# Layer 2's gate and up values by 26 products of a joint table, with GpSimd multiplying silu(gate) by up

## The chip, the core and the metric

The kernel runs on one core of a Trainium2 chip. The core's engines each work through their own instructions in order and wait for each other by semaphores: TensorE (PE, with its weight loads shown apart as PEld), VectorE (DVE), ScalarE (ACT), GpSimd (POOL) and SyncE (SP), whose queue issues all the DMA transfers spoken of here. Matrix products are written to PSUM and must be read out from there by VectorE or ScalarE. The metric is the device time of one execution in microseconds (us), all in float32.

## What is computed

x has 4 x 512 = 2048 rows of 512; the weights W_gate, W_up are 1376 x 512, W_down 512 x 1376, and each layer has its own. Cut to what matters:

```python
def layer1(x):                       # the k = 688 smallest |s| of a row become zero
    s = silu(x @ w_gate.T)
    s = zero_smallest_half(abs(s), s)
    return (s * (x @ w_up.T)) @ w_down.T
def layer2(x):
    return (silu(x @ W_gate.T) * (x @ W_up.T)) @ W_down.T
x = x + layernorm(layer1(layernorm(x)))
x = x + layernorm(layer2(layernorm(x)))
```

## The kernel before

The 2048 rows are 16 tiles of 128 rows. The program is one stretch of unrolled code; a scheduler of the language orders each engine's instructions by its own timeline estimate, within what `tc.issue_after` fixes by hand, and tile pools decide which tensors share memory: `big` has ten buffers (tag "b5"), `work` mostly two for a tag, and PSUM has the tags pa, px, py and pt with two banks each. A second path, `general`, is in the program for rows that the search could not settle and does not run here.

*Seven products.* Most matrix products use the scheme of seven products for a 2 x 2 x 2 block product (`Seven`, L134 to L168): sums of blocks are formed ahead (`stationary_sums` L117 for the weights' side, `moving_sums` L125 for the other), seven block products are accumulated in three banks, and while they run VectorE and ScalarE read partial sums out of the banks and add them up (`first`, `second`, `third`). A block product is two matmuls over 128 of the 512 inner values each (L144).

*Layer 1* runs over 8 units of two tiles (`units`, the loop over `j`): gate products (L433), up products by the seven-product scheme, a search for each row's threshold in six counting steps (L485 to L510 on ScalarE and VectorE), transposes of the masked values (`turns`, L607), sums of blocks (`down_sums` L618, on VectorE, tile D) and the down products (`finish`, which calls `downs` L234, with products p1 to p7), then the layer norm and the residual (`out_norm` L344). The units are overlapped: unit j's gate and up products carry the transposes of unit j-2 and the down products of unit j-3.

*The weights' sums* of the seven-product scheme are formed early in layer 1 by `presum` (L180): it loads blocks of a weight, forms four sums on VectorE with operations of 128 x 1280, and stores them to DRAM (`presums`). The first unit does this for layer 1's down weight ("a"), the second for layer 2's down, gate and up weights ("f", "g", "u"). At the end of layer 1 the sums of gate and up are loaded into the places that layer 1's weights held (tags wg, wu, and extra tiles).

*Layer 2* runs over 4 blocks of four tiles, 512 rows each. `Block.norm` normalizes and transposes a tile into xT; `Block.sums` forms the four sums of the moving side (4 operations of 128 x 512). The first 1280 of the 1376 hidden values go in five groups (HC = 5) of two slices of 128 hidden values: `Block.pair` (L682) makes gate and up values for a group, each with its own seven products of two matmuls of 256 columns, 28 matmuls in all, takes silu on ScalarE (L697, L700) and multiplies by up on VectorE (L698, L702). `Block.down_sums` (L721) forms the group's sums for the down product on GpSimd (four operations of 128 x 256, L119 to L122, tiles hTb and D). `Block.rest` does the last 96 hidden values with 14 matmuls. Then `Block.finish` does the down products for the block's tiles and the output norm. The norms and sums of the next block are issued behind the last group's last product (`block.mark`), under the down products.

*Around the change of layers* the program's order is: block 0's norms, the weights' loads, block 0's sums, the last unit's transposes, its block sums, its down products, and then the groups; TensorE's order as scheduled puts the first products of block 0 among the last unit's transposes and down products.

The lines that the steps below touch: L144, L154, L160, L161, L167, L168 (products and read-outs of `Seven`; L153 is ScalarE's first read-out), L260 and L266 (down products), L373 and L607 (transposes), L104 to L110 and L358, L359 (norms), L119 to L130 (sums), L206 and after (`presum`).

Of the kernel before, what the change touches and what calls it, by code (L numbers as in the profile page):

```python
# [29 lines left out]

@with_exitstack
def sandwich_kernel(
# [10 lines left out]
):  # L43

# [20 lines left out]
    HC = FULL // 2  # L65
    HF = HC * P
# [26 lines left out]
    presums = {k: dram.tile([4, P, HC * H2], F32, name=f"sum_{k}") for k in ("a", "f", "g", "u")}  # L93
# [86 lines left out]
    def presum(work, key, w_d):  # L180


        down = key in "af"
        bufs = dict(wd=3, hT=2)

        def load(r, c, tag, k):
            t = work.tile([P, HC * H2], F32, tag=tag, name=f"ps_{key}_{k}", bufs=bufs[tag])
            if down:
                src = w_d[r * HF : (r + 1) * HF, c * H2 : (c + 1) * H2]
            else:  # L190
                src = w_d[c * 2 * P : (c + 1) * 2 * P, r * HF : (r + 1) * HF]
            n = HC if down else 2
            nc.sync.dma_start(
                t.rearrange("p (k h) -> p k h", k=n), src.rearrange("(k p) h -> p k h", p=P)
            )
            return t

        def keep(k, t):
            nc.sync.dma_start(presums[key][k - 1], t)

        x = load(0, 1, "wd", "x") if down else load(1, 0, "wd", "x")
        y = load(0, 0, "wd", "y") if down else load(1, 1, "wd", "y")
        z = load(1, 1, "hT", "z") if down else load(0, 0, "hT", "z")
        w = load(1, 0, "wd", "w") if down else load(0, 1, "wd", "w")
        if down:
            nc.vector.tensor_sub(y, x, y)  # L206
        else:
            nc.vector.tensor_add(y, x, y)
        keep(1, y)
        nc.vector.tensor_sub(x, z, x)  # L210
        keep(3, x)
        if down:
            nc.vector.tensor_sub(z, z, y)
        else:
            nc.vector.tensor_sub(z, y, z)
        keep(2, z)
        nc.vector.tensor_sub(w, w, z)
        keep(4, w)

# [157 lines left out]
    class Unit:  # L377
# [205 lines left out]
        def turns(self, other=False):  # L583
# [4 lines left out]
            def turn(k, g0):  # L588
                nm = f"{self.nm}_{self.tiles[k]}"
                if g0 == 0:  # L590
                    if other:
                        if k == 0:
                            self.ends = self.work.tile(
                                [P, 2, P], F32, tag="S", name=f"he{nm}", bufs=1
                            )
                        t = self.big.tile([P, 2 * HC, P], F32, tag="b5", name=f"hT{nm}")
                        end = self.ends[:, k, :]
                    else:
                        t = self.work.tile([P, NI, P], F32, tag="hT", name=f"hT{nm}")
                        end = t[:, NI - 1, :]  # L600
                    self.hT.append((t, end[: isz[-1], :]))
                h, (hT, end) = self.p[k], self.hT[k]
                n = min(4, NI - g0)
                pt = psum.tile([P, 4, P], F32, tag="pt", name=f"ph{nm}_{g0}")
                for c in range(n):
                    i = g0 + c
                    nc.tensor.transpose(  # L607
                        pt[: isz[i], c, :], h[:, i * P : i * P + isz[i]], ident
                    )
                nf = n if g0 + n <= FULL else n - 1  # L610
                copy = nc.vector.tensor_copy if other and k else nc.scalar.copy
                copy(hT[:, g0 : g0 + nf, :], pt[:, :nf, :])
                if nf < n:
                    copy(end, pt[: isz[-1], nf, :])
# [39 lines left out]
    class Block:  # L654
# [15 lines left out]
        def sums(self):  # L670
            t = [
                self.big.tile([P, 2, 2, N2], F32, tag="b5", name=f"T{self.nm}_{self.b}_{q}")
                for q in range(2)
            ]
            self.right = moving_sums(
                nc.vector,
                *[half[:, :, cols] for half in self.xT for cols in (slice(N2), slice(N2, N))],
                t[0][:, 0], t[0][:, 1], t[1][:, 0], t[1][:, 1],
            )
            self.h = []  # L680

        def pair(self, a, lefts):  # L682
# [6 lines left out]
            sg = self.work.tile([P, 4, N2], F32, tag="w", name=f"sg{nm}", bufs=1)  # L689
            ms = []  # L690
            for k, left, c in zip("gu", lefts, (sg, h)):
                left = {p: w[:, :, ts(a, P)] for p, w in left.items()}
                m = Seven(f"{k}b{nm}", left, self.right, c[:, 1, :], c[:, 2, :], c[:, 3, :])
                m.first()
                ms.append(m)
            c11g, c11u = [m.second() for m in ms]
            nc.scalar.activation(sg[:, 0, :], c11g, AF.Silu)  # L697
            nc.vector.tensor_mul(h[:, 0, :], sg[:, 0, :], c11u)  # L698
            ms[0].third()
            nc.scalar.activation(sg[:, 1:, :], sg[:, 1:, :], AF.Silu)  # L700
            ms[1].third()
            self.mark = nc.vector.tensor_mul(h[:, 1:, :], sg[:, 1:, :], h[:, 1:, :]).ins  # L702

        def rest(self, left):

            n = I - 2 * HF
            nm = f"{self.nm}_{self.b}"
            t = self.work.tile([P, 4, N2], F32, tag="w", name=f"sgr{nm}", bufs=1)[:n]
            m = Seven(f"rb{nm}", left, self.right, t[:, 0, :], t[:, 1, :], t[:, 2, :])
            m.first()  # L710
            c11 = m.second()
            h = self.big.tile([P, N], F32, tag="b5", name=f"hTb{nm}_r")
            lo, hi = h[:n, :N2], h[:n, N2:]
            nc.scalar.activation(lo, c11, AF.Silu)
            m.third()
            nc.scalar.activation(hi, m.c12, AF.Silu)
            nc.vector.tensor_mul(lo, lo, m.c21)
            nc.vector.tensor_mul(hi, hi, m.c22)
            self.h.append(h)
# [17 lines left out]
        def finish(self, which, wr, final=False):  # L737

            pairs = []
            for q in which:  # L740
                last = lambda i, q=q: self.h[-1][: isz[-1], ts(q + 2 * i, P)]
# [23 lines left out]
    def layers(nm, general):  # L765
        with ExitStack() as sctx:
# [4 lines left out]
            def extra(k, layer):  # L771
                return [
                    wpool.tile([P, 2, 2 * Q], F32, tag=f"w{k}s{q}", name=f"w{k}s{q}{layer}{nm}")
                    for q in range(3)
                ]

# [23 lines left out]
            t1, t2, t4 = extra("u", 1)  # L800
# [23 lines left out]
            else:  # L824
                wr = last_rows(a_wd, 1)
                w_ds = dict(a=a_wd, f=f_wd, g=f_wg, u=f_wu)
                sums_at = {0: "a", 1: "fgu"}
                for j in range(NU):
# [22 lines left out]
                    for k in sums_at.get(j, ""):  # L851
                        presum(work, k, w_ds[k])
                steps = finish(units[-3:-1], wr)
# [14 lines left out]
            lefts, ws = [], []  # L868
            for k, w_d in (("g", f_wg), ("u", f_wu)):
                w = wpool.tile([P, NH, I], F32, tag="w" + k, name=f"w{k}2{nm}")  # L870
                s1, s2, s4 = [y[:, :, :HF] for y in extra(k, 2)]
                a11, a12, a21, a22 = [
                    w[:, 2 * c : 2 * c + 2, r * HF : (r + 1) * HF] for r in range(2) for c in range(2)
                ]
                for q, a in ((1, s1), (2, s2), (3, a21), (4, s4)):
                    nc.sync.dma_start(a, presums[k][q - 1].rearrange("p (k h) -> p k h", k=2))
                for a, c, r in ((a11, 0, 0), (a12, 1, 0), (a22, 1, 1)):
                    nc.sync.dma_start(
                        a,
                        w_d[c * 2 * P : (c + 1) * 2 * P, r * HF : (r + 1) * HF].rearrange(  # L880
                            "(k p) h -> p k h", p=P
                        ),
                    )
                nc.sync.dma_start(
                    w[:, :, 2 * HF :], w_d[:, 2 * HF :].rearrange("(k p) h -> p k h", p=P)
                )
                lefts.append(dict(p1=a11, p2=a12, p3=s4, p4=a22, p5=s1, p6=s2, p7=a21))
                ws.append(w)
            blocks[0].sums()
            if not general:  # L890
                for f in units[-1].turns():
                    f()
                units[-1].down_sums()
                for f in finish([units[-1]], wr):
                    f()
            wr = last_rows(f_wd, 2)
            t = work.tile([P, 3, 2, I - 2 * HF], F32, tag="S", name=f"wrs{nm}", bufs=1)
            rest = stationary_sums(
                nc.vector,
                *[w[:, 2 * c : 2 * c + 2, 2 * HF :] for w in ws for c in range(2)],  # L900
                t[:, 0], t[:, 1], t[:, 2],
            )
            for b, block in enumerate(blocks):
                last = b + 1 == len(blocks)
                for a in range(HC):
                    block.pair(a, lefts)
# [3 lines left out]
                block.rest(rest)  # L910
# [53 lines left out]
```

## Time and profile before

| | us |
|---|---|
| median of 3 runs | 867.67 (867.36 to 868.07) |
| the profiled execution | 867.17 |
| its span in the profile | 865.39 |
| layer 2, first product of block 0 alone to the span's end | about 445 to 865 |
| period of a block of layer 2 | 102.3 |

In the profile a line names engine, source line, operation, output <- inputs (partitions x elements), and count. A float32 matmul is two passes and counts twice: `x160` are 80 matmuls. The mean length of a matmul (380 ns for a pass of 256 columns) is its latency; passes follow each other more closely than that, so their spacing is read from the timeline. The costliest groups of layer 2 and some of the others:

```profile
L433 PE MATMUL pg<-wg,xT 128*128 128x456 f32 (+1 forms) x384 | 154.8, 549 | 0.2 <-ACT p L437 0.2
L144 PE MATMUL paub<-xTb,wu 128*128 128x256 f32 x160 | 41.3, 380 | 0.1
L144 PE MATMUL pagb<-xTb,wg 128*128 128x256 f32 x160 | 41.1, 379 | 0.0
L119 POOL TENSOR_TENSOR D<-hTb 128x256 f32<-128x256 f32 x20 | 14.6, 729 | 193.9 <-DVE hTb L702 193.9
L700 ACT ACTIVATE sg<-sg 128x768 f32<-128x768 f32 x20 | 16.9, 843 | 50.3 <-DVE sg L168 50.3
```

The figures behind the bar are the group's busy time, the mean of one in ns, and the idle time of the engine before them with what ended most of it.

### The profile page before, as it was taken

Reading aid. Unit: us, or ns where it says so; the run is one execution under the profiler, and the core shown is the slowest. Engines: PE = TensorE matmul, PEld = TensorE weight load, DVE = VectorE, ACT = ScalarE, POOL = GpSimd, SP = SyncE. Lnnn points to the kernel's source line nnn. Section 1 sums busy time; section 2 is a strip of 40 time slices with the busy share of each in tenths; the row PEclk is TensorE's granted clock in tenths of the full one; section 3 lists DMA queues with packets and bytes.
Section 4 is the critical chain, followed back from the end, with each engine's and each line's share of the span. In section 5 each row is a group of like instructions: output and inputs, shape, how many; then the busy total and the mean of one; then the engine's idle time right before and its main releaser. Section 6 shows DMA issues by size and latency. Waiting matters only on the chain.

```text
span 865.4 us, 10342 instructions
## 1 busy us (share of the span) xinstructions
PE 854.2 (99%) x3642; PEld 659.6 (76%) x3642; DVE 533.7 (62%) x1432; ACT 302.5 (35%) x601; POOL 98.8 (11%) x178
## 2 busy tenths in 40 slices
PE   9999999999999999999999999999999999999996
PEld 5556566767667676677888888888888888888885
DVE  5887787776949677667955445544436445454434
ACT  3465575647474755656111111011111112011100
POOL 1000000000000001000001220121301222012111
PEclk9999999999999999999999999999999999999999
DMA  9999414334233333387573005500054001430032
GB/s 334 372 329 347 177 55 123 122 100 163 67 116 108 123 122 104 100 323 262 169 242 119 0 1 170 189 2 0 18 183 159 1 0 46 153 125 1 0 100 100
DMA packets 60381, 112.96 MB, mean 131 GB/s; under 512 B 4705, under 2 KB 34529, under 8 KB 60321
## 3 DMA queue, kind: packets, MB, share of 16 engines
q1 hardware_dynamic: 60176, 111.95, 38.4%
q8 instruction: 31, 0.51, 0.2%
q14 instruction: 30, 0.24, 0.1%
q10 hardware_dynamic: 144, 0.26, 0.1%
HBM read 93.32 MB, written 18.87 MB: 130 GB/s over the span
## 4 chain that ended last, share of the span: by engine, by line
PE 51%; DVE 2%; ACT 1%; DMA 1%; issue 0%; POOL 0%; ACTq 0%; DVEq 0%
PE pxub L144 6%; PE pxgb L144 6%; PE pxdb L260 6%; PE paub L144 4%; PE pagb L144 4%; PE pydb L260 4%; PE pyub L144 4%; PE pygb L144 4%; PE padb L260 3%; PE pxd L260 2%; PE pyd L260 2%; PE pxrb L144 1%; PE pad L260 1%; ACT ja L485 1%; PE parb L144 1%; PE ptb L373 1%
## 5 line engine op out<-in xcount | busy, mean ns | idle before, releaser
L485 ACT ACTIVATE ja<-v,cur 128x1376 bf16<-128x1376 f32 x96 | 138.4, 1441 | 64.1 <-DVE cur L510 43.0
L433 PE MATMUL pg<-wg,xT 128*128 128x456 f32 (+1 forms) x384 | 154.8, 549 | 0.2 <-ACT p L437 0.2
L433 PEld LDWEIGHTS pg<-wg,xT 128*128 128x128 f32 x384 | 71.9, 190 | 62.7 <-issue 57.6
L144 PE MATMUL pau<-wu,xT 128*128 128x344 f32 x128 | 43.1, 453 | 0.0
L144 PE MATMUL paub<-xTb,wu 128*128 128x256 f32 x160 | 41.3, 380 | 0.1
L144 PE MATMUL pagb<-xTb,wg 128*128 128x256 f32 x160 | 41.1, 379 | 0.0
L144 PE MATMUL pxub<-T,wu 128*128 128x256 f32 x160 | 41.1, 379 | 0.0
L144 PE MATMUL pxgb<-T,wg 128*128 128x256 f32 x160 | 41.1, 379 | 0.0
L260 PE MATMUL pad<-wd_p,hT 128*128 128x256 f32 x160 | 38.9, 380 | 0.1
L437 ACT ACTIVATE p<-pg 128x456 f32<-128x456 f32 (+1 forms) x48 | 26.0, 543 | 36.4 <-PE pg L433 33.1
L260 PE MATMUL pydb<-wdb_p,D 128*128 128x256 f32 x160 | 37.3, 379 | 0.0
L490 DVE TENSOR_SCALAR low<-cur 128x2 int32<-128x2 f32 x48 | 7.9, 165 | 47.1 <-ACT ja L485 46.7
L260 PE MATMUL pxd<-wd_p,hT 128*128 128x256 f32 x160 | 36.8, 379 | 0.0
L119 POOL TENSOR_TENSOR D<-hTb 128x256 f32<-128x256 f32 x20 | 14.6, 729 | 193.9 <-DVE hTb L702 193.9
L260 PE MATMUL padb<-wdb_p,hTb 128*128 128x256 f32 x160 | 36.7, 379 | 0.0
L260 PE MATMUL pxdb<-wdb_p,hTb 128*128 128x256 f32 x160 | 36.2, 379 | 0.0
L260 PEld LDWEIGHTS pad<-wd_p,hT 128*128 128x128 f32 x160 | 29.9, 190 | 6.7 <-DMA wd_p<-in_L_attn_w_down_dram 0.5
L260 PEld LDWEIGHTS pxd<-wd_p,hT 128*128 128x128 f32 x160 | 30.4, 190 | 5.5 <-issue 0.4
L700 ACT ACTIVATE sg<-sg 128x768 f32<-128x768 f32 x20 | 16.9, 843 | 50.3 <-DVE sg L168 50.3
L110 POOL TENSOR_TENSOR rs_o<-ve_o,nhalf 128x1 f32<-128x1 f32 x16 | 11.5, 731 | 198.0 <-DVE ve_o L108 198.0
L144 PEld LDWEIGHTS paub<-xTb,wu 128*128 128x128 f32 x160 | 30.3, 190 | 4.5 <-ACT sg L697 0.4
L260 PEld LDWEIGHTS pxdb<-wdb_p,hTb 128*128 128x128 f32 x160 | 30.4, 190 | 4.2
(245 smaller groups left out, 1699.5 us busy)
## 6 DMA issues: line engine op xcount, KB each, us to landing
wd_p<-sum_a SPq DMA_DIRECT2D x28, 640.0 KB, 4.0
wd_p<-in_L_attn_w_down_dram SPq DMA_DIRECT2D x21, 640.0 KB, 3.9
wdb_p<-sum_f SPq DMA_DIRECT2D x16, 640.0 KB, 4.0
wdb_p<-in_L_ffn_W_down_dram SPq DMA_DIRECT2D x12, 640.0 KB, 3.9
xn<-in_x_dram SPq DMA_DIRECT2D x16, 256.0 KB, 4.1
xr<-in_x_dram SPq DMA_DIRECT2D x16, 256.0 KB, 4.1
x<-y SPq DMA_DIRECT2D x16, 256.0 KB, 3.1
xnb<-x SPq DMA_DIRECT2D x16, 256.0 KB, 4.1
```

The lines of the kernel that those rows point to most:

```text
L110: nc.gpsimd.tensor_tensor(rs, ve, nhalf, ALU.pow)
L119: eng.tensor_add(s1, a21, a22)
L144: nc.tensor.matmul(ps, self.left[k][:, c, :], self.right[k][:, c, :], start=first and c == 0, stop=c == 1, skip_group_check=not first,)
L260: nc.tensor.matmul(p[which], p[1](k, c), ws[k][:, c, :], start=first and c == 0, stop=c == HC - 1, skip_group_check=not first,)
L373: nc.tensor.transpose(pt[:, c, :], xn[:, ts(c, P)], ident)
L433: nc.tensor.matmul(pg, self.xT[:, i, c, :], wg[:, c, c0:c1], start=(c == 0), stop=(c == NH - 1),)
L437: nc.scalar.activation(p[:, c0:c1], pg, AF.Silu)
L485: nc.scalar.activation(junk, v, AF.Sign, bias=cur[:, 0, i : i + 1], accum_out=cur[:, 1, i : i + 1],)
L490: nc.vector.tensor_scalar(low, cur[:, 1, :], 0.0, None, ALU.is_gt)
L700: nc.scalar.activation(sg[:, 1:, :], sg[:, 1:, :], AF.Silu)
```

## The change

Layer 2's gate and up values of a group are no longer two times seven products of 2 x 2 x 2 blocks, but one table of 26 products for blocks of 4 (inner) x 2 (halves of the rows) x 2 (slices), found for gate and up together: each product is a single matmul of a sum of weight blocks (128 x 128) with a sum of blocks of x (128 x 256).

- `LEFT_SUMS` are the 18 sums of x's blocks, formed once for each block by `Block.sums` on VectorE, each 128 x 256. `RIGHT_SUMS` are the steps that turn a group's 16 weight blocks into 26, on VectorE in layer 1 (`weight_sums`): 17 steps for each group, 15 over two blocks (256 columns) and 2 over one, in units 0 to 4 for groups 4 to 0. Groups 4 to 1 are stored to DRAM (`w_ops`) and loaded at the end of layer 1; group 0's stay in memory (`area`).
- `PRODUCTS` lists, for each product, one of six banks, the index of the weight operand, that of the operand of x, and the outputs (0 to 3 gate, 4 to 7 up) to which the bank's content is added or subtracted after it. A bank used again accumulates. Outputs' first values are written by ScalarE, 8 for a group; the 18 additions are VectorE's.
- When a slice's gate is complete, ScalarE takes its silu (512 columns); GpSimd multiplies it by the up values (512 columns, two for a group) in place of VectorE's L698 and L702.
- The products of a block are ordered by hand (`issue_after`) in the order of the table.
- `Block.rest` does its 96 hidden values directly: 8 matmuls of 512 columns, one silu, one product on VectorE. Block 0's is issued before the last unit's down products.
- `presum` of "g" and "u" is gone, and the sums of the rest's weights.
- Block 0's sums are issued behind the last unit's block sums. The tile `he` gets a tag of its own; `sg` alternates between two tags, and the rest's hTb is in tag "junk".

The diff, cut to its core:

```diff
+LEFT_SUMS = (
+    "0 - 1", "2 - 6", "0 - 3", "5 - 6", "4 - 8", "6 - 7", "4 - 10", "5 + 9",
...
+RIGHT_SUMS = (
+    "2,16 = 2,12 - 6,8", "17,23 = 8,9 + 9,10", "18,19 = 11,11 + 17,23", "10,21 = 10,12 - 6,17",
...
+PRODUCTS = (
+    (0, 10, 17, "+2"), (1, 13, 23, "+6"), (2, 14, 24, "+1"), (0, 25, 21, "+6"), (1, 24, 8, "+2"),
+    (3, 3, 12, "+1"), (0, 11, 22, "+4"), (2, 23, 11, "-4-7"), (1, 8, 0, "+0"), (4, 7, 7, "+7"),
+    (3, 20, 13, "+3"), (5, 16, 3, "-7"), (1, 12, 6, "+4"), (0, 15, 2, "+0"), (4, 21, 5, "+5"),
+    (3, 1, 1, "+0"), (1, 4, 9, "+5"), (5, 22, 4, "+0+1"), (0, 2, 25, "+3"), (2, 19, 16, ""),
+    (1, 17, 20, "+1"), (4, 5, 15, "+4"), (0, 9, 14, "+7"), (2, 7, 19, "-6"), (5, 18, 10, ""),
+    (5, 3, 18, "+2"),
+)
...
+    def weight_sums(area, g):
+        def load():
+            for m in range(4):
+                w_d, f = (f_wg, f_wu)[m // 2], m % 2
+                cols = slice(f * HF + g * P, f * HF + (g + 1) * P)
+                nc.sync.dma_start(
+                    area[:, 4 * m : 4 * m + 4, :],
+                    w_d[:, cols].rearrange("(k p) h -> p k h", p=P),
+                )
...
+        def keep():
+            if g:
+                nc.sync.dma_start(w_ops[g - 1], area)
...
         def sums(self):
...
+            for text, t in zip(LEFT_SUMS, places):
+                ((a,), (b,)), (sa, sb) = terms(text)
+                signed_add(nc.vector, t, v[a], sa, v[b], sb)
+                v.append(t)
...
-        def pair(self, a, lefts):
+        def group(self, a, w):
...
+            for k, xv, wv, adds in PRODUCTS:
+                first = k not in banks
+                if first:
+                    tag = ("pa", "px", "py")[len(banks) % 3]
+                    banks[k] = bank(tag, f"{tag}b{nm}_{k}")[:, :N2]
+                with ExitStack() as order:
+                    if self.product is not None:
+                        order.enter_context(tc.issue_after(self.product))
+                    self.product = nc.tensor.matmul(
+                        banks[k], w[wv], self.left[xv], start=first, stop=True,
+                        skip_group_check=not first,
+                    ).ins
+                fresh = False
+                for o, s in form(adds).items():
+                    q, m = divmod(o, 4)
+                    c = (sg, h)[m // 2][:, m % 2 * 2 + q, :]
+                    if o in begun:
+                        add = nc.vector.tensor_add if s > 0 else nc.vector.tensor_sub
+                        self.mark = add(c, c, banks[k]).ins
+                    elif fresh:
+                        nc.vector.tensor_scalar(c, banks[k], float(s), None, ALU.mult)
+                    else:
+                        nc.scalar.mul(c, banks[k], float(s))
+                        fresh = True
+                    begun.add(o)
+                    left[m] -= 1
+                    f = m % 2
+                    part = slice(2 * f, 2 * f + 2)
+                    if m == f and not left[f]:
+                        nc.scalar.activation(sg[:, part], sg[:, part], AF.Silu)
+                    if not left[f] and not left[2 + f]:
+                        nc.gpsimd.tensor_mul(h[:, part], sg[:, part], h[:, part])
...
+        def rest(self, w):
+            ps = [bank(k, f"{k}rb{nm}")[:n, :] for k in ("pa", "px")]
+            for c, t in zip(ps, w):
+                for k in range(NH):
+                    nc.tensor.matmul(
+                        c, t[:, k, :], self.xT[k // 2][:, k % 2, :],
+                        start=k == 0, stop=k == NH - 1,
+                    )
+            h = self.work.tile([P, N], F32, tag="junk", name=f"hTb{nm}_r", bufs=1)
+            nc.scalar.activation(h[:n], ps[0], AF.Silu)
+            nc.vector.tensor_mul(h[:n], h[:n], ps[1])
...
-                sums_at = {0: "a", 1: "fgu"}
+                sums_at = {0: "a", 1: "f"}
...
+                    g = NG + 0 - 1 - j
+                    if 0 <= g < NG:
+                        for f in weight_sums(area, g):
+                            f()
...
                 for f in units[-1].turns():
                     f()
                 units[-1].down_sums()
+                last = nc.cur_bb.bb.instructions[-1]
+                with tc.issue_after(last):
+                    blocks[0].sums()
+                blocks[0].rest(w_rest)
                 for f in finish([units[-1]], wr):
                     f()
...
-                    block.pair(a, lefts)
+                    block.group(a, w_of[a * NP : (a + 1) * NP])
                     block.down_sums(a)
...
-                block.rest(rest)
+                if b or general:
+                    block.rest(w_rest)
```

## The prediction

> **What bounds the kernel now.** I read the page's first two parts, then windows of 20 us in layer 1, then the timeline of one group of layer 2, and last VectorE's timeline at the start of a block.
>
> ```profile
> PE 854.2 (99%) x3642; PEld 659.6 (76%) x3642; DVE 533.7 (62%) x1432; ACT 302.5 (35%) x601; POOL 98.8 (11%) x178
> PE   9999999999999999999999999999999999999996
> DVE  5887787776949677667955445544436445454434
> PEclk9999999999999999999999999999999999999999
> ```
>
> TensorE is busy in 854.2 of 865.4 us at full clock. The time is the number of matmul passes times their spacing; other engines count only where they make TensorE wait.
>
> ```profile
> 80.00:100.00 20.00, 20.00 (x59) 10.70 (x58) 19.93 (x40) 4.98 (x14) 0.00 (x0) 1.00 0.68 259
> 120.00:140.00 20.00, 19.84 (x67) 11.71 (x66) 17.75 (x48) 11.12 (x24) 0.65 (x2) 1.00 0.35 104
> ```
>
> Columns: window, sum, then PE, PEld, DVE, ACT, POOL busy, clock, DMA share, GB/s. VectorE was full from 80 to 100 us and TensorE still lost nothing: layer 1 has slack there. All waits of TensorE on others sum to about 3 us.
>
> ```profile
> 562.66 1.03 PE L144 MATMUL pxgb<-T,wg 128*128 128x256 f32 x4
> 563.53 1.03 PE L144 MATMUL pygb<-xTb,wgs 128*128 128x256 f32 x4
> 563.73 0.42 DVE L167 TENSOR_TENSOR sg<-sg,pxgb 128x256 f32<-128x256 f32 x1 [0.85 <-PE pxgb L144]
> ...
> 565.80 0.35 ACT L153 COPY hTb<-paub 128x256 f32<-128x256 f32 x1
> 566.12 1.03 PE L144 MATMUL pyub<-xTb,wus 128*128 128x256 f32 x4
> 566.32 0.42 DVE L167 TENSOR_TENSOR hTb<-hTb,pxub 128x256 f32<-128x256 f32 x1 [1.30 <-PE pxub L144]
> 566.98 1.03 PE L144 MATMUL pxgb<-T,wgs 128*128 128x256 f32 x4
> 567.71 0.96 DVE L702 TENSOR_TENSOR hTb<-sg,hTb 128x768 f32<-128x768 f32 x1
> ...
> 570.30 0.72 POOL L121 TENSOR_TENSOR hTb<-hTb 128x256 f32<-128x256 f32 x1
> 570.64 0.42 DVE L154 TENSOR_TENSOR hTb<-hTb,pxub 128x256 f32<-128x256 f32 x1 [1.11 <-PE pxub L144]
> ```
>
> Five products of four passes run from 562.66 to 566.98: 0.216 us a pass, 0.432 us for a float32 matmul of 256 columns (two passes). A result is read out 0.20 us after its slot's end (563.53 to 563.73), the read takes 0.42 us, and a bank is used again only four products (3.46 us) later.
>
> **The groups.** A group is 28 matmuls of 256 columns now (7 products x 2 x gate, up) and becomes 26. Five groups in four blocks: 20 x 2 x 0.432 = 17.28 us less.
>
> **The rest.** 14 x 0.432 = 6.05 us become 8 matmuls of 512 columns. No such matmul is in this trace; L433's passes of 456 columns are spaced by 0.385 us and those of 344 by 0.289, both 0.00084 a column, so 0.432 us a pass and 8 x 0.864 = 6.91. Four blocks: +3.46 us. A fixed part of a pass that a long one saves could only make it less. Net on TensorE: -13.82 us.
>
> **VectorE, ScalarE and GpSimd within a group** (now 26 x 0.432 = 11.23 us). VectorE: 18 adds from PSUM x 0.42 = 7.6 us, against 11 x 0.42 + 0.96 = 5.6. ScalarE: 8 first writes x 0.37 + 2 silus of 512 columns (768 columns took 0.84, a 512-column copy 0.58, so 0.6) = 4.2 us. GpSimd: its four sums of 256 columns, 4 x 0.73, plus two products of 512 columns. Such a product is not in the trace: below, 0.73 (it can't be shorter than half of it), above, twice, 1.45; VectorE's 512-column sums in SBUF take 0.68 against 0.42 for 256, a ratio of 1.6, which would make 1.18. I take 1.45: 5.8 us. All three lie under the 11.23 us and cost nothing while TensorE runs; if VectorE filled the group the price would be its excess, and it has 3.6 us spare. Behind a block's last group, GpSimd's product and sums end some 5 us after the group, while TensorE does the rest (6.9 us) and first asks for that group's hTb 6 to 8 us after: hidden.
>
> **The wait that is new: bank handoff.** Each of the 26 products goes into one of six rotating banks and must be read out before the bank's next product, since later products add onto it. By PRODUCTS the closest reuse is three places on: places 0 to 3, 1 to 4, 3 to 6; the next are four on. TensorE has two other products between, 0.864 us. The handoff is 0.195 (slot end to read) + 0.42 + the release back to TensorE. For the last, in the trace TensorE's first `pxdb` after a late VectorE result starts some 0.15 us after it. Sum 0.765 us, through ScalarE 0.72: it fits with 0.10 us to spare at distance three, 0.53 at four. Followed through all 26 places with these figures, a steady group stalls nowhere. What queues behind a late read is every later read on VectorE, which is in order.
>
> **The starts of blocks.**
>
> ```profile
> 554.90 0.30 DVE L106 BATCH_NORM_AGGREGATE mv_ob<-st_ob 128x2 f32<-128x6 f32 x2
> 555.17 0.42 DVE L154 TENSOR_TENSOR sg<-sg,pxgb 128x256 f32<-128x256 f32 x1
> 555.50 0.15 DVE L108 TENSOR_SCALAR ve_ob<-mv_ob 128x1 f32<-128x1 f32 x1
> 555.57 0.48 DVE L358 TENSOR_SCALAR yb<-yb,mv_ob 128x512 f32<-128x512 f32 x1
> ...
> 556.57 0.75 DVE L359 SCALAR_TENSOR_TENSOR yb<-yb,rs_ob,xrb 128x512 f32<-128x512 f32 x1
> ```
>
> The norms of the block before (L104 to L359) lie on VectorE among the first read-outs of the next block's first group. Before, a bank is asked for again seldom enough that 3 us of such work is hidden. Now a read that stands behind L358 and L359 (0.48, 0.75) is late by more than 0.53. Laying VectorE's new order against the 26 slots, TensorE waits at places 8 (0.37 us) and 14 (0.68): 1.05 us, three blocks, 3.2 us. Block 0's first group meets layer 1's last read-outs: places 6, 8 and 14, 1.0 us. Bounds: 0, and about 2.5 us a start (all of that norm work in the way), 10 us in all.
>
> **Layer 1 to layer 2.** Before, gate and up products of block 0 stand between unit 7's last transposes and its product p5 (437.5 to 438.9), and between p7 and p4 on the same bank (450.07 to 451.79). Now block 0's rest stands among the earlier transposes and the groups come after the unit. p5 then waits for copy and difference (0.58 + 0.42 + the ways, less what fills): 1.26 us; p4 on p7's bank, 0.75; the block's 18 sums, which are ordered behind the unit's last difference, make the first groups late by 0.5; a stall of 0.5 at that place goes. +2.0 us, bounds 0 and 5.
>
> **Layer 1.** Gone are gate's and up's precomputed sums (8 operations of 1.49 us, 8 loads and 8 stores of 0.66 MB, about 12 us of VectorE). New in units 0 to 4: 85 small operations on VectorE (0.34 us apart as back-to-back ones are, 29 us), 20 loads of 0.26 MB and 4 stores of 1.7 MB, on SP's queue. Their cover is the slack between a unit's search and its transposes: 0.4 us in unit 0, 10.6 in unit 1, then 25.7 to 54.9. Six microseconds a unit fit there except in unit 0, whose load also meets saturated DMA (share above 0.9 up to 40 us): +0.5 us, bounds 0 and 3. Layer 2's weights, 6.8 MB, load at the end of layer 1 as before; at the 246 GB/s of 400 to 420 us that is 28 us, and group 1 asks for the first of them about 40 us after the tiles come free. The block's sums, 18 x 0.42 against 4 x 0.68 us, lie under the 35 us of down products before.
>
> **Sum.** -13.8 + 3.2 + 1.0 + 2.0 + 0.5 = -7.1 us. From the profiled execution's 867.2 us (span 865.4 and 1.8 around it): 860.1. The median of the runs is 0.5 above that execution, and I put 860.3.
>
> **Rivals.**
>
> *All waits hidden* (chance 0.13). The scheduler may have laid the reads better than I follow: 867.2 - 13.8 = 853.4 us. For it: TensorE's waits were 3 us of 865 before. Against it: the slack per bank falls from over 2.6 us to 0.10.
>
> *The handoff doesn't fit* (0.20), the one on the slow side. Place: products 3, 4 and 6 of each group, 60 in all. From a handoff of 0.864 us on each loses the excess; at 0.98 the remaining 7.1 us are gone (60 x 0.118), and at 1.1 it is 60 x 0.236 = 14 us: 874. For it: my release is from few rows, and a read delayed behind another shifts all that follow. Against it: all three parts were read on this trace, and repeat to 0.02 us.
>
> *Starts and transition at twice the price or more* (0.07): +13 instead of +6.7, 866 to 868, no change.
>
> *VectorE in layer 1* (0.04): a search made late by sums that wait for their loads; up to 24 us if units 0 to 3 each slip by 6: 867 to 884. The window of 80 to 100 us speaks against it.
>
> *GpSimd's products lock VectorE out* (0.03). If a read-out had to wait for a GpSimd product, 40 products would each push a handoff by 0.73 - 0.53 to 1.45 - 0.10 us, 8 to 54 us: 868 to 914. The timeline speaks against it: L154 at 570.64 began inside POOL's L121 (570.30 to 571.02) and took the same 0.42 us. The Trainium skill, page "SBUF — State Buffer", section "Who interferes with whom", has a VectorE operation with two SBUF inputs and a GpSimd operation that reads SBUF exclude each other for a whole instruction. By that rule the 18 read-outs of a group, each with one input in PSUM, go free, which the row bears out; the block's 18 sums and L359, with two inputs in SBUF, could be held by up to one GpSimd product each, and no run here shows that.
>
> **Chances and range.** The forecast has the remaining 0.53, with a range of its own of 857 to 864. Faster by over 0.2% (below 865.9; 0.2% is about what can be told from no change): 0.53 + 0.13 = 0.66; within: 0.07; slower: 0.27. The range of 8 in 10 takes in the hidden case and the start of the slow one: 853 to 870.
>
> **What would show it.** Right: in a steady group the 26 products at 0.432 us, 11.2 us in all, TensorE busy near 840 us, waits of 1 us at block starts with VectorE as releaser, and a wait of over 1 us at unit 7's p5 on its difference. Wrong: a gap at places 3, 4 or 6 of every group (handoff); GpSimd's products above 1.45 us with down products waiting for hTb; the first group of block 0 starting later than in the kernel before by more than a few microseconds beyond the moved work; read-outs longer than 0.42 us while GpSimd multiplies.

## The result and the profile after

| | before | after |
|---|---|---|
| median, us (5 runs each) | 867.36 (866.33 to 868.07) | 858.40 (857.80 to 858.76) |
| ratio, 95% interval | | 0.9896 (0.9882 to 0.9911) |
| span of the profiled execution, us | 865.4 | 856.6 |

The change makes the kernel 1.0% faster; 860.3 us was forecast. The first part of the page of the changed kernel, and two rows of its groups:

```profile
PE 842.0 (98%) x3514; PEld 634.7 (74%) x3514; DVE 591.4 (69%) x1657; ACT 345.6 (40%) x713; POOL 151.4 (18%) x218
...
L837 POOL TENSOR_TENSOR hTb<-sg,hTb 128x512 f32<-128x512 f32 x40 | 50.8, 1270 | 133.2 <-DVE hTb L824 121.1
...
L824 DVE TENSOR_TENSOR sg<-sg,pxb 128x256 f32<-128x256 f32 x80 | 33.7, 421 | 19.3 <-PE pxb L814 17.3
```

TensorE is busy for 12.2 us less (854.2 to 842.0) and still in 98% of the span; the other three engines all got busier, and the kernel got faster. GpSimd's new product takes 1.27 us. Line numbers have moved: a product of a group is L814, its read-out L824 (VectorE) or L828 (ScalarE), a down product L368, the transposes L715, the norm's last steps L466 and L467.

**An account of TensorE.** For both kernels I took every matmul pass of the profiled execution, and subtracted from the time to the next pass's start the median spacing for that width (0.216 us for 256 columns, 0.429 for 512). What is left is waiting. Before: 7.3 us. After: 12.3 us. The groups give 17.3 us and the rest takes back 4 x (16 x 0.429 - 28 x 0.216) = 3.3, so -14.0 + 5.0 of waits + 0.25 behind the last matmul = -8.8 us, the change of the span. Almost every wait has 0.10 us added to it: the pass after a late one starts that much later than the median spacing. In the sums below it is included. These waits are more than the prediction's 3 us, which were only those that the profile puts down to another engine: of the 7.3 and 12.3 us, 2.4 and 2.3 lie in the first 10 us, at the first matmuls of the program.

A steady group, in the timeline of the changed kernel (start, duration, engine):

```profile
576.75 0.59 PE L814 MATMUL pab<-Ts,wu 128*128 128x256 f32 x2
577.18 0.59 PE L814 MATMUL pxb<-Ts,wg 128*128 128x256 f32 x2
577.45 0.42 DVE L824 TENSOR_TENSOR hTb<-hTb,pab 128x256 f32<-128x256 f32 x1 [1.38 <-ACT sg L828]
577.57 0.73 POOL L185 TENSOR_TENSOR D<-hTb 128x256 f32<-128x256 f32 x1
577.61 0.59 PE L814 MATMUL pab<-xTb,wg 128*128 128x256 f32 x2
```

TensorE's starts are 576.75, 577.18 and 577.61, each 0.43 us after the other, while VectorE reads out and GpSimd sums beside it. No group but the first of a block waits anywhere. In these rows `sg` holds gate values and `hTb` up values. The description of `PRODUCTS` above has their numbers wrong: by the code (`divmod(o, 4)`) outputs 0, 1, 4 and 5 are gate and 2, 3, 6 and 7 are up; 0 to 3 are the first half of the rows. The start of block 1:

```profile
554.81 0.48 DVE L466 TENSOR_SCALAR yb<-yb,mv_ob 128x512 f32<-128x512 f32 x1
555.21 0.42 DVE L824 TENSOR_TENSOR hTb<-hTb,pxb 128x256 f32<-128x256 f32 x1
555.67 0.30 PEld L814 LDWEIGHTS pxb<-T,area 128*128 128x128 f32 x2 [0.50 <-DVE hTb L824]
555.68 0.70 PE L814 MATMUL pxb<-T,area 128*128 128x256 f32 x2
555.87 1.41 DVE L467 SCALAR_TENSOR_TENSOR yb<-yb,rs_ob,xrb 128x512 f32<-128x512 f32 x2
...
557.19 0.42 DVE L824 TENSOR_TENSOR sg<-sg,pyb 128x256 f32<-128x256 f32 x1
...
557.64 0.38 ACT L828 ACTIVATE hTb<-pyb 128x256 f32<-128x256 f32 x1
...
558.14 0.42 DVE L824 TENSOR_TENSOR sg<-sg,pxb 128x256 f32<-128x256 f32 x1 [0.53 <-PE pxb L814]
558.48 0.42 DVE L824 TENSOR_TENSOR hTb<-hTb,pxb 128x256 f32<-128x256 f32 x1
558.95 0.70 PE L814 MATMUL pxb<-T,area 128*128 128x256 f32 x2 [0.41 <-DVE hTb L824]
```

Block 1's first product started at 551.96. The products at 555.68 and 558.95 are places 8 and 14 (counting from 0). Place 8 waits for a read-out that stood behind the norm step L466. Place 14 waits for the read-out at 558.48, which the norm holds by a chain: VectorE reads place 7's bank `pyb` at 557.19, behind L467; ScalarE reads the same bank only after that, at 557.64, and the read-out at 558.48 adds onto what ScalarE wrote. In VectorE's queue it also stands behind a read-out that had to wait for its own product until 558.14. And the last unit's down products:

```profile
442.79 0.70 PE L374 MATMUL pz<-wr,hT 96*128 96x256 f32 x2 [0.76 <-ACT hT L722]
443.49 2.02 PEld L368 LDWEIGHTS pyd<-wd_p,D 128*128 128x128 f32 x10 [0.40 <-DVE D L739]
449.90 2.43 PE L368 MATMUL pad<-wd_p,hT 128*128 128x256 f32 x10 [0.42 <-DMA wd_p<-in_L_attn_w_down_dram]
455.43 2.43 PE L368 MATMUL pxd<-wd_p,hT 128*128 128x256 f32 x10 [0.51 <-DVE y L396]
```

### The profile page after: what moved, and what is told of

Its sections match the earlier page's. It is cut to its first block, busy times and chain, and to the rows that moved or that the text cites. A ratio compares the mean times of both kernels' runs of the same rounds, so it can differ in the third digit from the quotient of the medians.

```text
span 856.6 us, 10602 instructions
## 1 busy us (share of the span) xinstructions
PE 842.0 (98%) x3514; PEld 634.7 (74%) x3514; DVE 591.4 (69%) x1657; ACT 345.6 (40%) x713; POOL 151.4 (18%) x218
## 5 line engine op out<-in xcount | busy, mean ns | idle before, releaser
L837 POOL TENSOR_TENSOR hTb<-sg,hTb 128x512 f32<-128x512 f32 x40 | 50.8, 1270 | 133.2 <-DVE hTb L824 121.1
L824 DVE TENSOR_TENSOR sg<-sg,pxb 128x256 f32<-128x256 f32 x80 | 33.7, 421 | 19.3 <-PE pxb L814 17.3
L835 ACT ACTIVATE sg<-sg 128x512 f32<-128x512 f32 x40 | 23.0, 622 | 47.9 <-DVE sg L824 47.9
L824 DVE TENSOR_TENSOR hTb<-hTb,pab 128x256 f32<-128x256 f32 x60 | 25.1, 419 | 22.2 <-ACT sg L828 11.0
L368 PE MATMUL pad<-wd_p,hT 128*128 128x256 f32 x160 | 38.9, 380 | 0.4 <-DMA wd_p<-in_L_attn_w_down_dram 0.4
L176 POOL TENSOR_TENSOR rs_i<-ve_i,nhalf 128x1 f32<-128x1 f32 x16 | 11.3, 711 | 154.1 <-DVE ve_i L174 93.8
L828 ACT ACTIVATE hTb<-pab 128x256 f32<-128x256 f32 x40 | 15.4, 384 | 56.7 <-PE pab L814 51.5
L368 PE MATMUL pydb<-wdb_p,D 128*128 128x256 f32 x160 | 37.8, 379 | 0.0
L368 PE MATMUL padb<-wdb_p,hTb 128*128 128x256 f32 x160 | 37.6, 380 | 0.2 <-DMA wdb_p<-in_L_ffn_W_down_dram 0.2
L368 PE MATMUL pxd<-wd_p,hT 128*128 128x256 f32 x160 | 37.1, 380 | 0.5 <-DVE y L396 0.5
L368 PE MATMUL pxdb<-wdb_p,hTb 128*128 128x256 f32 x160 | 36.1, 379 | 0.0
L368 PEld LDWEIGHTS pxd<-wd_p,hT 128*128 128x128 f32 x160 | 30.3, 190 | 6.6 <-DVE y L396 0.9
L368 PEld LDWEIGHTS pad<-wd_p,hT 128*128 128x128 f32 x160 | 29.7, 190 | 7.1 <-issue 1.2
L720 ACT COPY hT<-ph 128x512 f32<-128x512 f32 (+1 forms) x45 | 22.6, 511 | 28.4 <-PE ph L715 22.9
L210 PEld LDWEIGHTS pau<-wu,xT 128*128 128x128 f32 x128 | 23.8, 190 | 13.6 <-issue 4.6
L368 PEld LDWEIGHTS padb<-wdb_p,hTb 128*128 128x128 f32 x160 | 30.3, 190 | 4.7 <-DMA wdb_p<-in_L_ffn_W_down_dram 0.6
```

Of the source, the lines that this page charges most:

```text
L176: nc.gpsimd.tensor_tensor(rs, ve, nhalf, ALU.pow)
L210: nc.tensor.matmul(ps, self.left[k][:, c, :], self.right[k][:, c, :], start=first and c == 0, stop=c == 1, skip_group_check=not first,)
L368: nc.tensor.matmul(p[which], p[1](k, c), ws[k][:, c, :], start=first and c == 0, stop=c == HC - 1, skip_group_check=not first,)
L824: self.mark = add(c, c, banks[k]).ins
L828: nc.scalar.mul(c, banks[k], float(s))
L835: nc.scalar.activation(sg[:, part], sg[:, part], AF.Silu)
```

## The experiments

All but one are edits of the changed kernel. To read their times: the changed kernel, run once more on another occasion (below), gave 857.53 us, so two medians of one program can lie 0.9 us apart. The sum of TensorE's waits in each trace is given beside each, and the jitter of the spacings makes it uncertain by some 0.2 us; between those two traces it differs by 1.3 us too (12.3 and 11.0), 0.6 of it at two waits for weights that had not landed. What is steady from trace to trace are single waits (places 8 and 14 have 0.37 and 0.68 us in both), so the waits are compared place by place.

**The product back on VectorE.**

```diff
-                        nc.gpsimd.tensor_mul(h[:, part], sg[:, part], h[:, part])
+                        nc.vector.tensor_mul(h[:, part], sg[:, part], h[:, part])
```

> The change with its two products of silu and up done by VectorE again (512 columns in SBUF each, 0.68 us) and GpSimd left with its four sums. Theory (handoff with 0.10 us to spare at distance three, VectorE with a hole of about 1.3 us between the last read-out of a group and the first of the next): both products fall into or beside that hole, TensorE's steady groups stay at 11.2 us, and the time stays at 858.4 within 1.5 us; the part of the change that moved the product to GpSimd is then worth nothing. Rival (each product holds up the read-outs behind it): 40 x 0.15 to 0.58 us of waits, 864 to 882 us, with waits of TensorE on L824 in every group.

Measured: 859.00 us (858.52 to 860.86), span 857.1, waits 12.8 us, of which 1.4 are for a weight at 536 us (0.5 in the changed kernel); no steady group waits. The theory holds: with 26 products, VectorE has room for the two products, and giving them to GpSimd brings nothing that these runs resolve.

**That part alone, on the kernel before.**

```diff
-            self.mark = nc.vector.tensor_mul(h[:, 1:, :], sg[:, 1:, :], h[:, 1:, :]).ins
+            self.mark = nc.gpsimd.tensor_mul(h[:, 1:, :], sg[:, 1:, :], h[:, 1:, :]).ins
```

> The kernel before with one part of the change alone: GpSimd does L702 (the product of silu and up over 768 columns, 0.96 us on VectorE, some 1.9 us here by GpSimd's 1.27 for 512). Theory (that product is off TensorE's path on either engine): 867.4 within 1 us, like the undoing of this part in the changed kernel. Rival (GpSimd's later sums hold the block's first down products, or VectorE is freed for something that counted): 869 or more, or 866 or less.

Measured: 871.42 us (869.89 to 872.66), ratio 1.0045 (1.0031 to 1.0059), waits 11.2 us: my theory missed, it is slower. Of the 4.0 us of span, 1.9 lie at the ends of blocks 0 to 2, where TensorE's `pxdb` waits for a read-out of the rest. VectorE at that place, in the kernel before and then in this one:

```profile
526.68 0.41 DVE L167 TENSOR_TENSOR sgr<-sgr,pxrb 96x256 f32<-96x256 f32 x1
527.42 0.55 DVE L115 TENSOR_SCALAR xnb<-xnb,mv_ib,rs_ib 128x512 f32<-128x512 f32 x1 [0.34 <-POOL rs_ib L110]
```

```profile
528.93 0.55 DVE L115 TENSOR_SCALAR xnb<-xnb,mv_ib,rs_ib 128x512 f32<-128x512 f32 x1 [0.53 <-POOL rs_ib L110]
529.39 0.41 DVE L167 TENSOR_TENSOR sgr<-sgr,pxrb 96x256 f32<-96x256 f32 x1
529.86 2.43 PE L260 MATMUL pxdb<-wdb_p,D 128*128 128x256 f32 x10 [0.74 <-DVE sgr L167]
```

With the product gone from its queue the scheduler put L167 behind the norm step L115, which waits for GpSimd. In the changed kernel the last hidden values leave VectorE a single read-out, the product with `ps[1]`, and TensorE waits for it nowhere in the trace; there the same edit costs nothing that can be seen. Of the remaining 2.1 us, 1.2 are a longer wait at 72 us, behind a sum of `presum` that waited for its load, and 0.7 lie between 380 and 460 us. At 72 us the orders of all engines are those of the kernel before, so in this trace it is a late transfer; whether the edit has a part in that stays open.

**The handoff of a bank, measured.** The third and fourth product exchanged:

```diff
-    (2, 14, 24, "+1"),
     (0, 25, 21, "+6"),
+    (2, 14, 24, "+1"),
```

> The change with the third and fourth product exchanged, so that bank 0 is asked for again after one product (0.432 us) and no longer after two (0.864). If the handoff of a bank takes 0.72 to 0.77 us as the prediction summed it, TensorE waits 0.29 to 0.33 us once a group: 20 x 0.31 = 6.2 us, 864.6 us. If a handoff takes 0.98 us (the rival's point of no gain), 0.55 us a group, 869.4; if TensorE needs no more than the read-out itself (0.42 us), nothing, 858.4.

Measured: 862.11 us (862.01 to 862.54), span 860.2, waits 15.6 us. The second group of block 1:

```profile
564.11 0.59 PE L814 MATMUL pab<-T,wg 128*128 128x256 f32 x2
564.54 0.59 PE L814 MATMUL pxb<-T,wg 128*128 128x256 f32 x2
564.74 0.38 ACT L828 ACTIVATE hTb<-pab 128x256 f32<-128x256 f32 x1 [0.99 <-PE pab L814]
565.18 0.30 PEld L814 LDWEIGHTS pab<-Ts,wg 128*128 128x128 f32 x2 [0.44 <-ACT hTb L828]
565.18 0.70 PE L814 MATMUL pab<-Ts,wg 128*128 128x256 f32 x2
565.71 0.59 PE L814 MATMUL pyb<-T,wg 128*128 128x256 f32 x2
```

The bank `pab` is written from 564.11 to 564.54, read from 564.74 to 565.12, and its next product starts at 565.18; the product after that comes 0.53 later in place of 0.43. TensorE lost 0.31 us here and as much in 18 of the 20 groups: the handoff through ScalarE is 0.43 + 0.31 = 0.74 us, where the prediction's sum for that way was 0.72. All 18 make 5.6 us, but the waits grew by 3.3 only: at the starts of blocks 0, 1 and 3 TensorE now waits 0.0, 0.6 and 0.6 us in place of 0.5, 1.05 and 1.05 (each 0.6 includes 0.3 at the exchanged product), and some tenths differ elsewhere. A wait at an early place seems to be also time for VectorE to catch up; waits on one engine's queue don't simply add.

**Block 0's sums free to run early.**

```diff
-                with tc.issue_after(last):
-                    blocks[0].sums()
+                blocks[0].sums()
```

> The change without the order that holds block 0's sums behind the last unit's block differences. Theory: the sums run on VectorE in holes of the last search, group 0's first products are ready for TensorE as something to do between the last unit's transposes and down products, and some of the 2.9 us that TensorE waits between 440 and 460 us goes: 857.5, 856 to 858.4. Rival: the 18 sums (0.34 us each) stand in the way of the last search's chain on VectorE, the transposes come later and the time goes up by up to 6 us, 859 to 864.

Measured: 856.62 us (855.67 to 857.81), span 854.6, waits 10.1 us. The gain is where it was expected, 1.3 us for 2.9 between 440 and 460 us, but not by the way that was expected:

```profile
443.47 0.70 PE L374 MATMUL pz<-wr,hT 96*128 96x256 f32 x2 [0.78 <-ACT hT L722]
444.17 2.02 PEld L368 LDWEIGHTS pyd<-wd_p,D 128*128 128x128 f32 x10 [0.40 <-DVE D L739]
449.45 2.32 PE L368 MATMUL pxd<-wd_p,hT 128*128 128x256 f32 x10
451.61 2.32 PE L368 MATMUL pad<-wd_p,hT 128*128 128x256 f32 x10
454.20 2.32 PE L368 MATMUL pxd<-wd_p,hT 128*128 128x256 f32 x10
```

The waits at pz and pyd stay; what goes are those at 449.90 and 455.43 of the changed kernel. With the sums early, the scheduler put `pad` (p2) between the two products on `pxd`, so the second finds its bank read and `pad` finds its weights landed.

**Block 0's rest in its old place**, behind its groups:

```diff
-                blocks[0].rest(w_rest)
...
-                if b or general:
-                    block.rest(w_rest)
+                block.rest(w_rest)
```

> The change with block 0's rest behind its groups, as in the other blocks. Theory (the rest's 6.9 us fill a time in which TensorE has nothing else to do while the last search ends): 3 to 7 us slower, 861.4 to 865.4, with waits of TensorE on the last unit's transposes. Rival (it delays the transposes as much as it fills): 858.4 within 1 us.

Measured: 859.14 us (858.65 to 859.68), span 857.9, waits 13.5 us. A miss: nothing near 3 to 7 us. Without the rest the last unit's transposes and down products simply come earlier (pz at 436.95 for 442.79, with the same 0.92 us of wait); TensorE waits 0.3 us more at the transposes. The rest filled almost no idle time there. The other waits that this trace has more, 0.7 us in layer 1 and 0.4 at 834 us for a weight, lie where the program is the same.

**GpSimd's work raised.**

```diff
                         nc.gpsimd.tensor_mul(h[:, part], sg[:, part], h[:, part])
+                        nc.gpsimd.tensor_mul(sg[:, part], sg[:, part], h[:, part])
```

> The change with a second GpSimd product of 512 columns (1.27 us) behind each of the two of a group, its result used by nothing. GpSimd then has 4 x 1.27 + 2.9 = 8 us of work a group. Theory (GpSimd lies under TensorE's 11.2 us and, behind a block's last group, under the rest and the first down products): 858.4 within 1 us. Rival (the last group's sums are on the path): 2.5 us a block later, up to 10 us, 868.

Measured: 858.48 us (857.08 to 859.07), span 857.2, waits 12.7 us. As expected: 2.5 us more on GpSimd in a group are hidden, in the last group too.

**The norm's subtraction on GpSimd**, in layer 2:

```diff
-            nc.vector.tensor_scalar(y, y, mv[:, 0:1], None, ALU.subtract)
+            (nc.gpsimd if nm[:1] == "b" else nc.vector).tensor_scalar(y, y, mv[:, 0:1], None, ALU.subtract)
```

> The change with the subtraction of the mean in layer 2's output norms (L466, 0.48 us, four for a block of which two stand among the next block's first read-outs) on GpSimd. Theory (the waits at products 8 and 14 of blocks 1 to 3 are VectorE's norm work ahead of the read-outs): of 2.7 us of waits at the three starts more than half goes, 856.8 us. Rival (the waits come from L467 or from the handoff itself): the starts keep their 2.7 us, 858.4; or L467 now waits for GpSimd with read-outs queued behind it, up to 3 us more.

Measured: 861.72 us (860.24 to 863.72), span 859.7, waits 13.5 us: slower, by the second rival. The scheduler now has L467 of the earlier tiles among the next statistics:

```profile
554.55 0.72 DVE L467 SCALAR_TENSOR_TENSOR yb<-yb,rs_ob,xrb 128x512 f32<-128x512 f32 x1
554.79 1.91 POOL L466 TENSOR_SCALAR yb<-yb,mv_ob 128x512 f32<-128x512 f32 x1 [1.75 <-ACT sg L828]
555.27 0.39 DVE L824 TENSOR_TENSOR hTb<-hTb,pab 128x256 f32<-128x256 f32 x1
555.72 0.70 PE L814 MATMUL pab<-T,area 128*128 128x256 f32 x2 [0.90 <-DVE hTb L824]
```

TensorE waits 1.16 us at place 6 for a read-out that began at 555.27, behind L467. The subtraction takes GpSimd 1.56 to 1.91 us against 0.48 on VectorE, and the last output tile is later by 1.8 us behind the last matmul. It confirms what holds the starts (norm work ahead of read-outs), but this edit moves the wait and doesn't take it away.

**The last norm steps deferred.** The subtraction and the last step of the two norms that end a block are put into a list, and done later; first, one behind each of the next block's first two groups:

```diff
+        if defer:
+            late.append(apply)
+        else:
+            apply()
...
                     block.group(a, w_of[a * NP : (a + 1) * NP])
+                    if late:
+                        with tc.issue_after(block.mark):
+                            late.pop(0)()
```

> The change with the subtraction and the last step (L466 and L467, 1.15 us) of the two output norms that end a block put behind the last read-out of the next block's first and second group, one each, where VectorE has a hole of 1.4 us. Theory (the waits at blocks' starts are these operations ahead of read-outs): of 2.7 us of waits at the starts of blocks 1 to 3 at most 0.6 stays, 856.3 us, 855.5 to 857. Rival (statistics or the handoff itself make them): 858.4.

Measured: 858.74 us (857.88 to 858.89), span 856.9, waits 12.2 us: no gain. The waits at the starts are gone, as the theory said, but 0.6 us has come up at place 6 of groups two and three, six times. VectorE and GpSimd there:

```profile
561.93 2.67 POOL L847 TENSOR_TENSOR hTb<-sg,hTb 128x512 f32<-128x512 f32 x2 [7.07 <-DVE hTb L834]
563.00 0.48 DVE L471 TENSOR_SCALAR yb<-yb,mv_ob 128x512 f32<-128x512 f32 x1
563.57 1.58 DVE L472 SCALAR_TENSOR_TENSOR yb<-yb,rs_ob,xrb 128x512 f32<-128x512 f32 x1
564.68 1.06 POOL L185 TENSOR_TENSOR D<-hTb 128x256 f32<-128x256 f32 x1
565.08 0.41 DVE L834 TENSOR_TENSOR hTb<-hTb,pab 128x256 f32<-128x256 f32 x1
565.54 0.70 PE L824 MATMUL pab<-T,wg 128*128 128x256 f32 x2 [0.33 <-DVE hTb L834]
```

L472 is the old L467: 1.58 us here, 0.75 where GpSimd doesn't work on tiles. It began while GpSimd's product ran, and ended 0.55 us after that product had; then GpSimd's next sum took 1.06 in place of 0.73. The hole was long enough for 0.48 + 0.75, not for 0.48 + 1.58.

**Deferred to behind the fifth group**, where TensorE does the rest and no bank is needed soon:

```diff
-                    if late:
+                    if a == HC - 1:
                         with tc.issue_after(block.mark):
-                            late.pop(0)()
+                            while late:
+                                late.pop(0)()
```

> As the kernel with the deferred last steps of two output norms, but both now behind the last read-out of the next block's fifth group, where TensorE does 6.9 us of the rest and then down products and no bank is asked for again quickly. Theory (in the deferred kernel L467 took 1.58 us in place of 0.75 because a GpSimd product ran beside it, and held the third product's read-out; the waits at the starts themselves were gone): the waits at blocks' starts stay gone and none comes in groups two and three, 858.4 - 2.6 = 855.8 us. Rival (norm work costs its time wherever it stands among the read-outs or the down products): 857.5 to 858.5, with new waits behind group five.

Measured: 855.40 us (855.09 to 855.85), span 854.0, waits 9.4 us. Only 0.13 us, the small matmul that counts bad rows, is left at the starts of blocks 1 to 3. L467 still runs against GpSimd here (0.91 to 1.21 us), and nobody waits for it. Of the 9.4 us, 0.9 are a wait for a weight at 632 us, and 0.3 stand at place 6 of block 2's third group, which the kernel below with the same edit does not have; its cause stays open.

**Both gains together, and the changed kernel again**, in one session with the last:

> The same with the free sums of block 0. The two save different waits: 858.4 - 1.8 - 2.6 = 854.0 us; if they don't add, 855.5 to 857.

> The changed kernel itself, on the same chip as the two above: 858.4 within 0.8 us by every theory; it tells what two runs of one program differ by.

The changed kernel: 857.53 us (857.31 to 858.12), waits 11.0. Both edits: 853.99 us (853.94 to 854.57), ratio to the kernel before 0.9846 (0.9832 to 0.9859), span 852.2, waits 7.5. They add. The first try at both, with the deferred steps behind groups one and two:

> The deferred norm steps and the free sums of block 0 together. If both gains are separate waits of TensorE they add: 858.4 - 1.8 - 2.1 = 854.5 us; if one uncovers another wait, 855.5 to 857.

It gave 858.02 us (857.66 to 858.37), span 856.5, waits 11.9: the starts' gain was given back in groups two and three, and layer 1 waited 0.4 us more than in the kernel with the free sums alone. The page of the best version, in which TensorE waits as little as before the change:

```profile
PE 840.1 (99%) x3514; PEld 635.3 (75%) x3514; DVE 597.7 (70%) x1657; ACT 345.3 (41%) x713; POOL 155.0 (18%) x218
```

## Why the prediction was right

By its own steps, forecast against the account of TensorE's passes:

| step | forecast, us | measured, us |
|---|---|---|
| groups, 28 to 26 matmuls | -17.3 | -17.3 |
| rest, directly | +3.5 | +3.3 |
| starts of blocks 1 to 3 | +3.2 | +2.7 |
| start of block 0 | +1.0 | +0.5 |
| layer 1 to layer 2 (420 to 460 us) | +2.0 | +1.8 |
| layer 1 (to 420 us) | +0.5 | -0.2 |
| other down products | 0 | +0.1 |
| behind the last matmul | 0 | +0.25 |
| sum | -7.1 | -8.8 |

**Groups and handoff.** No steady group waits, as the reserve of 0.10 us at distance three said. The exchange of two products shows it from the other side: at distance two the wait is there, and to within 0.02 us as long as the handoff that was summed from three rows makes it. One reading in that sum was loose: after a late read-out TensorE starts 0.05 us later (527.08 to 527.14 in the kernel before, 565.12 to 565.18 here), not 0.15; the other 0.10 is what the pass behind a late one loses. So as long as nothing is late the reserve at distance three is nearer 0.2 us than 0.10. The rival that it doesn't fit is out, and that GpSimd locks the read-outs out is out too: L824 takes 0.42 us beside L837 and alone.

**Starts.** Blocks 1 and 3 wait at places 8 (0.37 us) and 14 (0.68), those places and, to 0.01 us, that much. Block 2 waits 0.57 in place of 1.05, at one place: the small matmul of `count_bad` comes between and VectorE's order differs there. That norm work ahead of the read-outs is the cause is shown by moving it: the waits go with it. Block 0 waits at places 6 (0.27) and 14 (0.18), and not at 8. So the rival that all waits are hidden (853.4 us) did not come; the kernel with both edits, at 853.99 us, shows that nearly all of them could be.

**The transition** has the right sum by parts that came differently. p5 with pz before it waits 1.29 us (forecast 1.26), but 1.02 of it at pz, for ScalarE's copy, and only 0.27 at p5, for the difference; p4 on p7's bank waits 0.78 (0.75). The late sums cost only 0.10, and 0.69 at `pad`, for a weight that had not landed (0.33 in the kernel before), and 0.19 at the rest's first product were not foreseen. In return waits of 1.3 us in the kernel before are gone, where the prediction counted 0.5. That this term fits to 0.2 us is in part luck.

**GpSimd.** 1.27 us lies between the bounds of 0.73 and 1.45; the value of 1.45 was too high, the estimate of 1.18 by VectorE's ratio nearer. It didn't matter, and the raised load shows by how much: 2.5 us more in a group are still covered.

**What was off** is the size of three small terms, all too dear: the start of block 0, layer 1, and block 2's start, together 1.7 us. For layer 1 the account finds no cost of the new sums: waits there fell by 0.2 us, with 0.43 us at 126 us that the kernel before has and the changed kernel does not, and 0.6 us more at the transposes near 398 us. But over the traces of kernels with the changed layer 1 the same sum runs from 4.7 to 6.0 us (5.5 in the kernel before), so these tenths are not told from noise.

## What to carry to other kernels

When a kernel is bound by one engine, count that engine's slots for the gain, and then follow each shared buffer (here a PSUM bank) from its last write through its read-out to its next write, against the slots in between: 0.74 us of handoff against 0.86 of other products is enough, and against 0.43 it is not. The places to look for what the gain gives back are the seams, where other work stands in the same in-order queue ahead of a read-out; moving that work to where no buffer is wanted back won 2.1 us here; giving a part of it to another engine cost some 3 us. An order constraint written by hand should be tried without: here it cost 1.4 us (855.40 to 853.99 without it, in one session), through the order of two down products.

## What the runs showed of the hardware

A VectorE operation with tiles of SBUF as two inputs and a GpSimd operation on SBUF tiles don't run at once: L467 took 1.58 us beside a product of GpSimd and 0.75 without. With one tile and scalars it happens too. The next block's norm step, in the changed kernel, first beside GpSimd's sums and then, at 532.76, alone, where it took 0.55:

```profile
521.09 0.73 POOL L186 TENSOR_TENSOR D<-D,hTb 128x256 f32<-128x256 f32 x1
521.16 0.94 DVE L181 TENSOR_SCALAR xnb<-xnb,mv_ib,rs_ib 128x512 f32<-128x512 f32 x1 [0.56 <-POOL rs_ib L176]
521.78 0.91 POOL L187 TENSOR_TENSOR hTb<-hTb 128x256 f32<-128x256 f32 x1
```

L181 and then L187 are each held by the other (0.94 for 0.55, 0.91 for 0.73). The subtraction L466 (L471 there), with one tile and one scalar, took 1.48 us beside a GpSimd product in the kernel with the steps behind the fifth group, and 0.48 alone. In the rows of the first try at deferring, L471 kept its 0.48 us: it began 0.2 us before the first of the two GpSimd products ended, and there the second product took 1.38 us in place of 1.27. Read-outs with one input in PSUM are not held (0.42 us with and without). The blocked time shows as a longer operation, not as a wait. The Trainium skill, page "SBUF — State Buffer", section "Who interferes with whom", says that a VectorE operation with two SBUF inputs contends with a GpSimd operation that reads SBUF, that one in a mode that uses both ports, which `tensor_scalar` can enter, contends with GpSimd too, and that one with at most one SBUF input outside those modes does not. The traces agree on all three kinds, though no row says which mode L181 and L466 ran in. The prediction had it for L467 as a possibility without a row; it decided the first try at deferring the norm's steps.
